# A deformable-attention block and three attention layers: a third folding step moved to DMA, and the MLP's first pixel block in seven products

## The chip, the cores and the metric

One core of one Trainium2 chip runs one program. The metric is device time in microseconds (us) of that core. A time is the median of several executions; a profile is one execution recorded by the hardware profiler. Engines: TensorE (PE, matmul), VectorE (DVE), ScalarE (ACT), GpSimd (POOL), SyncE (SP). Everything is float32.

## The reference, cut to what matters

The input is x, 2 x 512 x 32 x 32. Four layers follow one another: layer 0 is deformable attention and an MLP, layers 1 to 3 are attention layers on the same pixels. The change lies in layer 0 and in its MLP. There each of 8 groups of 64 channels has 64 sampled points (8 x 8) at learnt offsets, and the bias between each of 1024 pixels and each point comes from a small network:

```python
pos = grid_q[:, :, None, :] - grid_kv[:, None, :, :]          # 16 groups x 1024 pixels x 64 points x 2
bias = jnp.sign(pos) * jnp.log1p(jnp.abs(pos))
bias = jax.nn.relu(bias @ cpb_w1 + cpb_b1)                    # 2 -> 128
bias = jax.nn.relu(bias @ cpb_w2 + cpb_b2)                    # 128 -> 128
bias = (bias @ cpb_w3 + cpb_b3).reshape(b, GROUPS, H * W, Hd * Wd)
sim = jnp.einsum('bhid,bhjd->bhij', qh, kh) + bias
attn = jax.nn.softmax(sim, axis=-1)
...
x = x + out                                                   # attention, projected
xn2 = _bn(x, bn2_g, bn2_b)
h1 = gelu(einsum('bchw,oc->bohw', xn2, mlp_w1) + mlp_b1)      # 512 -> 2048
return x + einsum('bchw,oc->bohw', h1, mlp_w2) + mlp_b2       # 2048 -> 512
```

## The kernel before, in words

**Tiles and steps.** Layer 0 works on 8 tiles t (2 images x 4 pairs of groups). A tile has 128 points (two groups of 64) and 1024 pixels, and is done in 32 steps of four points, so the loop in `layer0` has 256 steps i. A step has four turns k = 0 to 3, each for one quarter (`part`) of the 128 hidden channels of the bias network, in the order 1, 0, 3, 2. Steps are numbered here within a tile too: "phase" is i modulo 32.

**What one turn issues.** `first` (L526, DVE) makes the first hidden layer of one point, 128 channels x 1024 pixels, from two tables; it works seven points ahead (`AHEAD`) in a ring of eleven buffers, eight of which are slices of the weight tile `wa`. `second` (L543, PE) multiplies the four points of the step by one quarter of `cpb_w2`, four points side by side in four groups of 32 columns, and ACT evicts with relu (L552). After the second and fourth turn, `joined` (L557, DVE) adds two quarters, so that after the next step's second turn a step has two arrays, and a DMA issued by POOL (L832) adds one to the other. A step is then one array of 128 partitions: 4 points x 32 sums of channels.

**Folding by DMA, two steps at a time.** At each even step a POOL DMA (L825) adds the odd partitions of an even step's array to its even ones, and at the odd step an SP copy (L827) and a POOL DMA (L829) put the odd step's two halves on top of each other in the freed odd partitions. Two steps are now one array of 8 points x 16 sums. `third` (L571, PE) sums those over the channels into `sim`, the scores of a tile: four such arrays per call, one in each group of 32 columns, for both halves of the pixels. A call covers 8 steps and comes 11 steps after the first of them: at phases 11, 19, 27 and, in the next tile, 3. The last of the four is followed by `scores` (L579) and by a new side queue.

**The side queue** `behind` holds what else a tile needs, as generators that are advanced by one `yield` at the second and fourth turn of each step: `finish(t)` (softmax of the scores, transposes `pt` L594 and `pa` L614), `offsets(t + 2)` (projection `pq` L328, 36 taps on ACT summed by six DVE reduces L353, then the tables), and `samples(t + 1)` (bilinear sampling `pk`, key and value products `pkv`, `pvo` L484, `pb` L488, `simbias` L490). The order of issue on each engine is the program's order (`in_order`). Matmul outputs outside of `sim` come from three PSUM buffers (`zt`), which `second` uses too.

**The end of layer 0 and the MLP.** `finish_last` does the softmax of the last tile in halves and the last projection of the image (`project_out` L629, `add_out` L639). `layers` begins with the MLP in 8 blocks of 256 pixels. Blocks 1 to 7 take seven products of half-size matrices for each eight (Strassen's scheme, Winograd's form: `lefts` and `rights` form the sums on DVE, `products` multiplies in PE with 128 columns, `combined` adds up). Block 0 is a plain product with 256 columns (`pmp`, L136), under which DVE forms the sums of w1 and w2 for the others.

Of the kernel before, what the change touches and what calls it, by code (L numbers as in the profile page):

```python
# [12 lines left out]
F32 = mybir.dt.float32  # L13
# [6 lines left out]
P = 128  # L20
# [12 lines left out]
RCH = 8  # L33
# [47 lines left out]
def kernel(ctx: ExitStack, tc: tile.TileContext, a: dict, out: bass.AP):  # L81
# [55 lines left out]

    def layer0(l0, fold_d, t2_b, o2_b):
# [5 lines left out]
        h2p = l0.enter_context(tc.tile_pool(name="att_h2", bufs=6))  # L144
        h2j = l0.enter_context(tc.tile_pool(name="att_h2j", bufs=3))
        h2b = l0.enter_context(tc.tile_pool(name="att_h2b", bufs=3))
        h2q = l0.enter_context(tc.tile_pool(name="att_h2q", bufs=3))
        dram = l0.enter_context(tc.tile_pool(name="l0dram", bufs=1, space=DRAM))
# [17 lines left out]
        qkw = h2j.tile([P, 2, NPAIR, P], F32, name="qkwbd", tag="h2")  # L166
# [58 lines left out]
        for w in (w3, w3_4):  # L225
            nc.gpsimd.memset(w, 0.0)
# [5 lines left out]
        def bias_weights():  # L232
# [3 lines left out]
            few = one.tile([P, 26], F32, name="few")  # L236
# [68 lines left out]
            nc.vector.tensor_scalar(w3[:, 24:32], w3[:, 24:32], w3sign[:, 1:2], None, ALU.mult)  # L305
            magnitude(b2h, w3_of)
# [14 lines left out]
        def offsets(t):  # L321
# [49 lines left out]
            if t:  # L371
                yield
            act = actbd[t % 2]
# [26 lines left out]
            yield  # L400
            sgn = two.tile([P, 2, 32], F32, name="sgn")
# [19 lines left out]
        def samples(t):  # L421
# [36 lines left out]
            yield  # L458

# [12 lines left out]
            yield  # L472
            pkv = zt([P, 2, P], "pkv")
# [9 lines left out]
            pvo = zt([P, C], "pvo")  # L483
            nc.tensor.matmul(pvo, values, ow, start=True, stop=True)  # L484
            vos[t] = vop.tile([P, C], F32, name="vo")
            nc.scalar.copy(vos[t], pvo)
            pb = zt([P, 1], "pb")
            nc.tensor.matmul(pb, kq, b1q[:, pr : pr + 1], start=True, stop=True)  # L488
# [4 lines left out]
        NCH = 2 * NR // RCH  # L493
        tabs_of = {}

        def load_tabs(c):
# [4 lines left out]
            for ax in range(2):  # L501
                src = slog_d[t, ax].rearrange("(q r) i -> q r i", q=4)
                tab = two.tile([P, 2, RCH, 32], F32, name=f"tab{ax}")
                q, r = rc % 2 * 2, rc // 2 * RCH
                nc.sync.dma_start(out=tab, in_=src[q : q + 2, r : r + RCH, :].partition_broadcast(P))
                tabs_of[c].append(tab)
# [8 lines left out]
        def first(p):  # L515

            chunk, quad = divmod(p, 2 * RCH)
            quad, point = divmod(quad, RCH)
            if quad == 0 and point == 0:
# [9 lines left out]
                in0=tx[:, quad, point, :].unsqueeze(1).to_broadcast([P, H, W]),  # L529
                in1=ty[:, quad, point, :].unsqueeze(2).to_broadcast([P, H, W]),  # L530
# [5 lines left out]
        def second(i, h1s, part):  # L536
# [13 lines left out]
            ring = h2q if part % 2 else h2b if part else h2j if i % 2 else h2p  # L550
            h2 = ring.tile([P, HW], F32, name="h2", tag="h2")
# [10 lines left out]
        def third(sim, r, h2s, fours=(), halves=range(2)):  # L562

            for half in halves:
                n = slice(half * HALF, (half + 1) * HALF)
                ways = [(quad, w3[:, 24 - r : 56 - r], h2) for quad, h2 in enumerate(h2s)]
# [16 lines left out]
        def finish(t, sim):  # L583
# [4 lines left out]
            simb = two.tile([P, HW], F32, name="simb", tag="simb")  # L588
# [10 lines left out]
            at = two.tile([P, 8, P], F32, name="at", tag="simb")  # L599
# [10 lines left out]
            nc.vector.tensor_tensor(atv, atv, sm.unsqueeze(2).to_broadcast([P, 16, NJ]), ALU.mult)  # L610
            yield
# [29 lines left out]
        def finish_last(sim, eights, fours):  # L641
# [3 lines left out]
            table(AF.Exp)  # L645
            pps = [zt([P, HW], "pp")]
            project_out(pps[0], b, 0, range(2))
            simb = two.tile([P, HW], F32, name="simb", tag="simb")
# [4 lines left out]
            pt = zt([P, 8, P], "pt")  # L653
            ptv = pt.rearrange("p i (g j) -> p (i g) j", j=NJ)
            mx = two.tile([P, 16], F32, name="mx")
            at = two.tile([P, 8, P], F32, name="at", tag="simb")
# [156 lines left out]
        for i in range(steps):  # L813
            for k, part in enumerate((1, 0, 3, 2)):
# [18 lines left out]
                if k % 2:  # L833
                    next(behind, None)
# [1391 lines left out]
```

## Time and profile before

| What | us |
|---|---|
| Median of three runs | 3383.11 (3380.47 to 3383.16) |
| The profiled execution, its own time | 3381.55 |
| Its span, first to last instruction | 3379.8 |
| PE busy, DVE busy, ACT busy, POOL busy | 3348.8, 2654.9, 1804.6, 464.7 |
| The loop of 256 steps | 57.7 to 2003.0 |
| One tile of the loop, from 501.68 to 742.01 | 240.33 |
| End of layer 0 (`finish_last`) | 2003.0 to 2042.1 |
| MLP block 0, then block 1 | 2043.39 to 2099.20, then to 2149.36 |

The granted clock of TensorE was 1.00 in every stretch that was looked at. A busy time is that in which an engine works on at least one instruction; waiting for a semaphore is idle time, and it is listed with the instruction that ended it. Instructions of PE overlap in the pipeline, so the time that one adds is read from the distance of starts, not from its own duration. A step of the loop that has nothing but its own `second` takes 6.87 us on PE (54.93 us for 512 instructions, 64 to a step: every float32 matmul is two instructions in the trace).

### The profile page before, as it was taken

Reading aid. Unit: us, or ns where it says so; the run is one execution under the profiler, and the core shown is the slowest. Engines: PE = TensorE matmul, PEld = TensorE weight load, DVE = VectorE, ACT = ScalarE, POOL = GpSimd, SP = SyncE. Lnnn points to the kernel's source line nnn. Section 1 sums busy time; section 2 is a strip of 40 time slices with the busy share of each in tenths; the row PEclk is TensorE's granted clock in tenths of the full one; section 3 lists DMA queues with packets and bytes.
Section 4 is the critical chain, followed back from the end, with each engine's and each line's share of the span. In section 5 each row is a group of like instructions: output and inputs, shape, how many; then the busy total and the mean of one; then the engine's idle time right before and its main releaser. Section 6 shows DMA issues by size and latency. Waiting matters only on the chain.

```text
span 3379.8 us, 61349 instructions
## 1 busy us (share of the span) xinstructions
PE 3348.8 (99%) x24861; PEld 1611.8 (48%) x24861; DVE 2654.9 (79%) x3458; ACT 1804.6 (53%) x2764; POOL 464.7 (14%) x563
## 2 busy tenths in 40 slices
PE   9999999999999999999999999999999999999999
PEld 4333333333333333333333337999953443687777
DVE  6999999999998899999999964464446566665656
ACT  4866867867866667867867651121226235122221
POOL 0222222222222122222222210000000000000000
PEclk9999999999999999999999999999999999999999
DMA  5676676676665476676676651000100000000111
GB/s 167 147 150 139 142 155 139 138 152 141 151 146 121 105 151 142 146 149 137 146 150 148 140 141 57 11 11 14 48 4 13 27 29 20 7 7 1 32 32 36
DMA packets 147284, 320.33 MB, mean 95 GB/s; under 512 B 31664, under 2 KB 77360, under 8 KB 146224
## 3 DMA queue, kind: packets, MB, share of 16 engines
q0 software_dynamic: 56880, 199.79, 31.1%
q1 hardware_dynamic: 88816, 111.81, 10.8%
q8 instruction: 198, 3.24, 0.4%
q10 hardware_dynamic: 1296, 4.72, 0.4%
q14 instruction: 94, 0.77, 0.1%
HBM read 71.46 MB, written 10.83 MB: 24 GB/s over the span
## 4 chain that ended last, share of the span: by engine, by line
PE 79%; DVE 15%; issue 4%; ACT 2%; DMA 0%; POOL 0%; DVEq 0%; SPq 0%; ACTq 0%; POOLq 0%
PE z L543 35%; DVE wa L526 6%; PE pw L1392 6%; PE pma L136 5%; PE pmb L136 4%; DVE h L557 4%; PE pmv L1392 4%; PE score L1571 3%; PE pv L1583 3%; PE pm L1392 3%; PE score L1392 3%; DVE h L526 2%; PE pmp L136 2%; PE pp L629 2%; PE pmt L1392 1%
## 5 line engine op out<-in xcount | busy, mean ns | idle before, releaser
L543 PE MATMUL z<-wa,cpb_w 128*32 128x512 f32 x11904 | 1779.1, 593 | 6.7 <-DVE simbias L490 3.4
L552 ACT ACTIVATE h<-z,b2h 128x1024 f32<-128x1024 f32 x1024 | 1134.9, 1114 | 529.1 <-PE z L543 505.7
L543 PE MATMUL z<-h,cpb_w 128*32 128x512 f32 x4480 | 986.3, 593 | 3.3 <-ACT h L552 2.2
L543 PEld LDWEIGHTS z<-wa,cpb_w 128*32 128x32 f32 x11904 | 493.0, 110 | 883.6 <-issue 804.2
L526 DVE CUSTOM_DVE_ANT_1 wa<-tab,tab 128x1024 f32<-128x1024 f32 x744 | 879.4, 1219 | 33.9 <-PE z L543 33.9
L557 DVE SCALAR_TENSOR_TENSOR h<-h,turn,h 128x1024 f32<-128x1024 f32 x512 | 654.7, 1279 | 8.8 <-ACT h L552 8.5
L543 PEld LDWEIGHTS z<-h,cpb_w 128*32 128x32 f32 x4480 | 256.3, 110 | 335.0 <-issue 292.0
L832 POOL DMA_DIRECT2D h<-h x255 | 227.2, 891 | 1062.4 <-DVE h L557 715.2
L526 DVE CUSTOM_DVE_ANT_1 h<-tab,tab 128x1024 f32<-128x1024 f32 x280 | 333.5, 1219 | 10.5 <-PE z L543 10.4
L1214 ACT COPY p<-pma 128x128 f32<-128x128 f32 x70 | 18.6, 266 | 305.5 <-PE pma L136 305.5
L1572 ACT ACTIVATE p<-score 128x512 f32<-128x512 f32 x256 | 130.0, 624 | 81.2 <-PE score L1571 80.4
L1206 DVE TENSOR_TENSOR upper<-pma,p 128x256 f32<-128x256 f32 x70 | 29.5, 422 | 163.4 <-ACT p L1214 163.3
L825 POOL DMA_DIRECT2D h<-h x126 | 109.6, 870 | 336.7 <-DMA h<-h 332.5
L829 POOL DMA_DIRECT2D h<-h x126 | 119.5, 948 | 133.0 <-DMA h<-h 126.7
L1604 DVE TENSOR_TENSOR acc<-acc,p 128x1024 f32<-128x1024 f32 x96 | 111.1, 1219 | 19.0 <-ACT p L1572 18.8
L1571 PE MATMUL score<-q,k 64*128 64x512 f32 x512 | 120.7, 604 | 1.1 <-DVE gm L1088 1.1
L1583 PE MATMUL pv<-p,vT 128*64 128x512 f32 x512 | 116.5, 598 | 0.0
L513 ACT ACTIVATE tab<-tab,pc 128x512 f32<-128x512 f32 x126 | 96.2, 763 | 0.0
L1392 PE MATMUL pmv<-wa,hc 128*128 128x256 f32 x384 | 89.7, 380 | 0.3 <-DVE u L1415 0.3
L347 ACT ACTIVATE products<-qpad,pc 128x64 f32<-128x64 f32 x252 | 85.5, 408 | 0.0
L1571 PEld LDWEIGHTS score<-q,k 64*128 64x128 f32 x512 | 47.3, 186 | 70.3 <-issue 54.9
L1392 PEld LDWEIGHTS pmv<-wa,hc 128*128 128x128 f32 x384 | 72.6, 190 | 14.2 <-issue 2.8
(451 smaller groups left out, 3708.5 us busy)
## 6 DMA issues: line engine op xcount, KB each, us to landing
h<-h POOLq DMA_DIRECT2D x255, 512.0 KB, 5.0
h<-h POOLq DMA_DIRECT2D x252, 256.0 KB, 4.8
tab<-slog_d SPq DMA_DIRECT2D x128, 256.0 KB, 4.5
h<-h SPq DMA_DIRECT2D x126, 256.0 KB, 2.3
r<-d SPq DMA_DIRECT2D x24, 256.0 KB, 3.5
xt<-in_xt SPq DMA_DIRECT2D x8, 512.0 KB, 7.8
wa<-in_mlp_w SPq DMA_DIRECT2D x4, 1024.0 KB, 7.8
wb<-in_mlp_w SPq DMA_DIRECT2D x16, 256.0 KB, 5.5
```

What stands on the lines that cost most here:

```text
L136: nc.tensor.matmul(pm, w, m, start=(k == 0), stop=(k == len(pairs) - 1))
L526: nc.vector._custom_dve(TENSOR_ADD_SAT, out=h1.rearrange("p (y x) -> p y x", x=W), in0=tx[:, quad, point, :].unsqueeze(1).to_broadcast([P, ...
L543: nc.tensor.matmul(z[point * 32 : point * 32 + 32, n], cpb_w2[:, lo : lo + 32], h1s[point][:, n], start=True, stop=True,)
L552: nc.scalar.activation(h2, z, AF.Relu, bias=b2h[:, part : part + 1])
L557: nc.vector.scalar_tensor_tensor(h2, h2, turn[:, part // 2 : part // 2 + 1], parts.pop(part + 1), ALU.mult, ALU.add)
L829: nc.gpsimd.dma_start(out=joins[i - 3][1:P:2], in_=joins.pop(i - 2)[1:P:2], accum_op=ALU.add)
L832: nc.gpsimd.dma_start(out=joins[i - 1], in_=other, accum_op=ALU.add)
L1392: nc.tensor.matmul(out, stationary(l, k), moving(r, k), start=start and k == 0, stop=k == nk - 1, skip_group_check=not start,)
L1571: nc.tensor.matmul(sc, ks[m][r, s * P : (s + 1) * P], qs[m][r, n], start=True, stop=True)
L1572: nc.scalar.activation(p[:, part], sc, AF.Exp, scale=64 ** -0.5)
L1583: nc.tensor.matmul(pv[half][part * 64 : part * 64 + 64], vt[s % 4][:, lo : lo + 64], lps[s, half][:, part, :], start=(s == 0), stop=(s == 7),)
L1604: nc.vector.tensor_add(acc[half], acc[half], ps[s, half])
```

## The change

Three things are changed together.

1. **A third fold.** Except for the last 16 steps of the last tile, four steps are put into one array of 16 points x 8 sums. Every step's array is folded once by POOL (256 KB); the first of four is folded again by POOL (128 KB), and each of the other three is brought in by an SP copy and a POOL DMA of 128 KB each. `third` is called once for 16 steps, with another weight tile (`w3_16`) but in the same eight matmuls, 20 steps after the first of them (phases 20 and, in the next tile, 4), ahead of the turn's `second`. The arrays that stay live (`h2p`, six) are slices of a new tile `bridge`, the passing ones (`h2j`) are four instead of three, two of them in `bridge`. A table load now brings 16 points of one quarter instead of 8 of two.
2. **The side queue's turns.** `finish`, `offsets` and `samples` have two more `yield`s each, `pb` moves into the PSUM buffer of `pvo` and ahead of it, and the queue starts half a step later.
3. **The MLP's block 0** goes the way of the others, in seven products. The sums of w1 are formed in `finish_last`, a column block after each of the eight `add_out`s, in slices 0 to 5 of `bridge`; the normalized pixels and their sums are made in slices 6 and 7, before the last exponentials. `finish_last` has two PSUM tiles for its transposes instead of one. The sums of w2 move into the second half of block 0; the loads and constants at the start of `layers` move behind its first lines.

```diff
+        h2p = cycle([bridge[:, k, :] for k in range(6)])
+        h2j = cycle([bridge[:, 6, :], bridge[:, 7, :], *(one.tile([P, HW], F32, name=f"h2j{k}") for k in range(2))])
...
+            quarter = few[:, 26:28]
+            for k in range(2):
+                nc.vector.tensor_reduce(quarter[:, k : k + 1], ident[:, 2 + k : P : 4], AX.X, ALU.add)
+                nc.vector.scalar_tensor_tensor(eighth, quarter[:, k : k + 1], 8.0, eighth, ALU.mult, ALU.add)
+            nc.vector.tensor_scalar(w3_16[:, 16:32], row[:, 0:16], eighth, 0.0, ALU.add, ALU.is_equal)
+            nc.vector.tensor_scalar(w3_16[:, 16:32], w3_16[:, 16:32], w3sign[:, 1:2], None, ALU.mult)
...
-            pvo = zt([P, C], "pvo")
-            nc.tensor.matmul(pvo, values, ow, start=True, stop=True)
+            pvo = zt([P, HW], "pvo")
+            pb = pvo[:, C : C + 1]
+            nc.tensor.matmul(pb, kq, b1q[:, pr : pr + 1], start=True, stop=True)
+            nc.tensor.matmul(pvo[:, :C], values, ow, start=True, stop=True)
...
-                if i < steps - 2:
-                    if i >= 2 and i % 2 == 0 and k == 0:
-                        nc.gpsimd.dma_start(out=joins[i - 2][0:P:2], in_=joins[i - 2][1:P:2], accum_op=ALU.add)
-                    if i >= 3 and i % 2 and k == 0:
-                        nc.sync.dma_start(out=joins[i - 3][1:P:2], in_=joins[i - 2][0:P:2])
-                    if i >= 3 and i % 2 and k == 3:
-                        nc.gpsimd.dma_start(out=joins[i - 3][1:P:2], in_=joins.pop(i - 2)[1:P:2], accum_op=ALU.add)
...
-                due = i - 11
-                if k == 1 and due >= 0 and due % 8 == 0:
+                due = i - 20
+                if k == 1 and 0 <= due < LAST and due % 16 == 0:
                     t, r = divmod(due, NR)
                     if r == 0:
                         sim = ps_s.tile([P, HW], F32, name="sim")
-                    third(sim, r, [joins.pop(due + j) for j in range(0, 8, 2)])
-                    if r == NR - 8:
+                    third(sim, r, [joins.pop(due + j) for j in range(0, 16, 4)], wide=True)
+                    if r:
...
+                if 0 <= i - 2 < LAST:
+                    j = (i - 2) % 4
+                    whole, own = joins[i - 2 - j], joins[i - 2]
+                    if k == 0:
+                        nc.gpsimd.dma_start(out=own[0:P:2], in_=own[1:P:2], accum_op=ALU.add)
+                    if k == 3 and j == 0:
+                        nc.gpsimd.dma_start(out=own[0:P:4], in_=own[2:P:4], accum_op=ALU.add)
+                    if k == 3 and j:
+                        nc.sync.dma_start(out=whole[j:P:4], in_=own[0:P:4])
+                if k == 1 and i - 1 in parts:
+                    other = joined(parts.pop(i - 1), 2)
+                    nc.gpsimd.dma_start(out=joins[i - 1], in_=other, accum_op=ALU.add)
+                j = (i - 3) % 4
+                if k == 1 and 0 <= i - 3 < LAST and j:
+                    nc.gpsimd.dma_start(
+                        out=joins[i - 3 - j][j:P:4], in_=joins.pop(i - 3)[2:P:4], accum_op=ALU.add
+                    )
...
+            pts = [zt([P, 4, P], "pt") for _ in range(2)]
             pps = [zt([P, HW], "pp")]
             project_out(pps[0], b, 0, range(2))
...
+            right_sums()
+            pps.append(ps_s.tile([P, HW], F32, name="pp", tag="sim"))
...
+            pps += [zt([P, HW], "pp") for _ in range(2)]
             for half, n in enumerate(halves):
-                for m in range(3):
-                    project_out(pps[m], b, m, range(NPAIR) if m == 2 else [pr], [half])
+                for m in range(CC):
+                    project_out(pps[m], b, m, range(NPAIR) if m >= 2 else [pr], [half])
                     add_out(b, m, n, pps[m])
+                    next(left_sums)
...
-            xn = normed(0)
-            hid = one.tile([P, HID // P, BLK], F32, name="hid")
-            for c in range(MC):
-                for m in (MC + c, c):
-                    pm = bank("pmp")[:, :BLK]
-                    accumulate(pm, [(w1[:, k, m * P : (m + 1) * P], xn[:, k, :]) for k in range(CC)])
-                    nc.scalar.activation(hid[:, m, :], pm, AF.Gelu, bias=col("mlp_b1", m))
-                form1(nc.vector, slice(c * P, (c + 1) * P))
...
-            for blk in range(1, NBLK):
+            nc.gpsimd.memset(ones, 1.0)
...
+            later = [form2(slice(c * P, (c + 1) * P)) for c in range(2)]
+            for blk in range(NBLK):
...
+                    if blk == 0 and c >= 4:
+                        advance(later[0])
...
+                if blk == 0:
+                    drain(chain(*later))
```

## The prediction, made before the changed kernel was run

> **What bounds the kernel now.** I read the page first (busy times, then the chain), then busy time by stretch, then the groups of one tile, then the two timelines side by side, and PE's waits last.
>
> ```profile
> PE 3348.8 (99%) x24861; PEld 1611.8 (48%) x24861; DVE 2654.9 (79%) x3458; ACT 1804.6 (53%) x2764; POOL 464.7 (14%) x563
> ...
> PE 79%; DVE 15%; issue 4%; ACT 2%; DMA 0%; POOL 0%; DVEq 0%; SPq 0%; ACTq 0%; POOLq 0%
> ```
>
> PE is the bound: every matmul removed should shorten the span. DVE's 15% of the chain is the warning: 79% is an average over two different stages. By stretch (span, then busy us of PE, PEld, DVE, ACT, POOL, clock, DMA share):
>
> ```profile
> 501.68:742.01 240.33, 239.07 (x2172) 74.52 (x2168) 232.99 (x213) 179.46 (x249) 56.01 (x66) 1.00 0.67 144
> 2000.00:2043.40 43.40, 39.08 (x141) 15.57 (x133) 12.97 (x17) 10.54 (x40) 0.94 (x4) 1.00 0.31 109
> 2043.39:2099.20 55.81, 55.81 (x258) 48.62 (x259) 24.68 (x48) 8.81 (x17) 4.01 (x7) 1.00 0.25 83
> 2099.20:2149.36 50.16, 50.16 (x451) 50.10 (x450) 23.26 (x75) 8.92 (x25) 2.31 (x4) 1.00 0.03 9
> ```
>
> In a tile of the loop DVE works 232.99 of 240.33 us, 6 us less than PE: a second bound close behind. The two MLP blocks differ by 5.65 us of pure PE. The end of layer 0 has 4.3 us of idle PE.
>
> ```profile
> L571 PE MATMUL sim<-h,w 128*32 128x512 f32 x64 | 7.6, 592 | 0.0
> ...
> 556.43 1.90 PE L571 MATMUL sim<-h,w 128*32 128x512 f32 x16
> ...
> 563.83 2.36 DVE L526 CUSTOM_DVE_ANT_1 wa<-tab,tab 128x1024 f32<-128x1024 f32 x2 [3.15 <-PE z L543]
> ...
> 668.18 2.36 DVE L526 CUSTOM_DVE_ANT_1 wa<-tab,tab 128x1024 f32<-128x1024 f32 x2
> 670.45 1.28 DVE L557 SCALAR_TENSOR_TENSOR h<-h,turn,h 128x1024 f32<-128x1024 f32 x1
> 671.64 2.36 DVE L526 CUSTOM_DVE_ANT_1 wa<-tab,tab 128x1024 f32<-128x1024 f32 x2
> ```
>
> The first line is the work to be halved. The DVE lines give its pace: 2.27 us from start to start for two `first`, 1.19 for a `joined`, so 2 x 2.27 + 2 x 1.19 = 6.92 us a step against PE's 6.87. Where PE inserts something, DVE waits for a free buffer (3.15).
>
> ```profile
> PE z L543 <- ACT h L552: 5.4, 11, 0.7
> PE z L543 <- DVE simbias L490: 4.5, 8, 0.6
> ...
> PE pmp L136 <- POOL xn L1224: 1.3, 1, 1.3
> ...
> PE pt L662 <- DVE mx L663: 0.9, 1, 0.9
> PE pp L629 <- DVE x L639: 0.8, 1, 0.8
> PE sim L571 <- ACT simb L652: 0.8, 1, 0.8
> ...
> PE pt L679 <- ACT at L669: 0.5, 1, 0.5
> ```
>
> **The thirds: what goes.** 31 calls in the loop become 16, each still eight matmuls (16 records). PE's step starts give the price: a step with a `third` and nothing else takes 8.58 us, a plain one 6.87, so 1.71 (the group's 1.90 overlaps its neighbours). 15 x 1.71 = **-25.7 us**, about 3.4 a tile.
>
> **Does DVE allow it?** I take as lead the start of PE's first `second` of a step less the end of the DVE instruction that made its fourth point. It is capped at 5.45 plus what PE inserts in the step before, by the ring of eleven; a plain step costs it 0.06, each of the six reduces 0.95, and what PE inserts adds to it. In the tile at 501 it reads 6.3 at phase 12, then 5.35, 4.4, 3.45, 2.5, 2.0, 1.9, 1.8 at phase 19, where a `third` lifts it: PE never caught up. With the new phases the balance is: 5.0 at phase 4; `third`, `scores` and `pt` there (3.76 + 1.16) lift it, the cap cuts it back to 5.4; `pa` and `pq` (1.1, 2.0) at 9 and 10 make good the softmax's 1.5 on DVE; 5.4 at phase 13. The reduces fall at 12 to 17, so 4.4, 3.5, 2.5, 1.6, 0.6, and 0.1 at 19 (`po` adds 0.42); no `third` at 11 helps any more, the next is at 20, and then it is 1.6. So PE catches up for about a step: 0.3 us each in six tiles, and 0.5 in the first, where the lead is 0.7 to 1.1 already at steps 8 to 11. **+2.3 us** (0 to 12, if it starts 1.5 lower). A tile then asks 236 us of PE, still over DVE's 233.
>
> **The third fold: what it adds.** For four steps: before 4 DMAs of 512 KB, 4 of 256 by POOL, 2 of 256 by SP; after 4 of 512, 4 of 256 and 4 of 128 by POOL, 3 of 128 by SP. So 12 POOL issues for 8, 3968 KB for 3584, and a DMA share near 0.75 for 0.67. POOL's row:
>
> ```profile
> L832 POOL DMA_DIRECT2D h<-h x33 | 29.4, 892 | 131.8 <-DVE h L557 78.1 <-DMA h<-h 26.0 <-DVE simbias L490 7.8
> ...
> h<-h POOLq DMA_DIRECT2D x255, 512.0 KB, 5.0
> h<-h POOLq DMA_DIRECT2D x252, 256.0 KB, 4.8
> ```
>
> At 0.9 us an issue POOL needs 2.7 of 7.4 us a step. The page SBUF — State Buffer of the Trainium skill (section "SBUF: two separate sides") speaks against more of this: POOL writes the descriptors of its DMAs through ports that a DVE operation in a two-port mode locks, and the page tells of 620 ns becoming 3100. Three issues of 3.1 would be 9.3 us a step: some 240 x 1.7 = +410 us. The row has a mean of 0.89 with DVE busy 97%, so I count 0.9. What counts more is POOL's order. At turn 0 it waits for the last step's 512 KB to land, to fold it; the next 512 KB addition, the 128 KB addition and (one step in four) the second fold are queued behind. The cycle is an issue of 0.87 plus a landing of 5.0, 5.9 us, under PE's shortest step of 6.87. The last 128 KB lands some 4.5 steps after its step began, against 5.25 for the `third` that needs it: 5 us to spare, 2 where DVE is late. The buffers of `h2j` come back after five steps, with about as much. A 128 KB addition isn't in the trace: between the SP copy's 2.3 and the 4.8 of 256 KB; I take 4, the nearer row's kind. SP's copies wait for a fold with the tables' loads queued behind, and these have four steps' time. **+1 us** (0 to 15, one a `third`).
>
> **The side queue.** `pb` no longer holds a PSUM buffer alone until DVE reaches `simbias`: -4 of the 4.5 us of that wait. The 5.4 us for ACT sit mostly at phase 5 (two waits of 0.4 and 0.5), where table load, tables and exponentials meet; the extra turns thin them out, but the table load comes nearer to the tables' scaling. I count 0 (-5 to +3). **-4 us.** The six small DVE operations for `w3_16`, 0.2 each by the small rows, lie in the start under PE's folding of weights: **+0.5** (0 to 1.2, uncovered).
>
> **The end of layer 0.** Separate transposes' tiles remove half of the 0.9 and the 0.5; `pp` waits no more for `add_out` (0.8); xn is ready in time (1.3): its POOL work (2.2) starts when the second half of `third` has read the slice, and DVE's 1.7 of sums follow before the first reciprocal. Against this, the first projection gets the third PSUM buffer, which ACT frees at 2004.3 where PE stood ready at 2003.0: +1.4. The w1 sums, 1.5 us behind each `add_out` of 0.8 on DVE, take 8 x 2.3 = 18.4 us against PE's 17.8 of projection; w1 landed at 2015, ten us before. DVE ends 2 us after PE, and block 0 first asks DVE after 3 us of products. Without the slack it would be these 2. **-1.7 us** (-3.1 to +1).
>
> **Block 0.** The page TensorE: Matmul & The Clock Gate of the skill (section "Back-to-back issue gap") speaks against halves of 128 columns: it gives some 81 ns a matmul at 128 columns and 131 at 512, about 98 at 256 by a line between (my estimate), so 448 x 81/98 against 256: 45% more, +25 us. The rows say 50.16 / 448 = 112 ns against 55.81 / 256 = 218, near half: block 1 is the same work, and I take it. The sums of w2 (8 operations of some 1.2 us on DVE) fit in 25 us of idle DVE; w2 landed 15 us after its issue, and in the new order its last chunk comes when the fifth column block is done, without PE waiting. **-5.65 us** (-5.7 to -3).
>
> **Sum.** -25.7 + 2.3 + 1 - 4 + 0.5 - 1.7 - 5.65 = -33.2 from the profiled execution's 3381.55 (span 3379.8 and 1.75 around it) is 3348.3; that execution is 1.6 below the median, so 3350.
>
> **The rivals.**
> - *Half of the loop's gain comes back as waits.* For it: the lead at 0.1, and DVE, POOL and DMA all fuller. Against it: PE asks 3 us a tile more than DVE. Six tiles at 1.7 more and fifteen `third`s at 0.4: +16, **3366**.
> - *All idle PE in the loop goes.* A tile has 1.26 of it, 9.5 in all instead of 4; no wait at the first projection, no lost lead: -9, **3341**.
> - *Slower: POOL's cycle becomes the bound.* Fold, addition and landing are one chain, and each step now has it. A tenth of the 512 KB additions land after more than 6.7 us, those beside a fold or a table load; 128 KB more in flight, at the 0.8 between 512 and 256 KB by rows, is 0.4: 7.1, a cycle of 8.0 against 7.6 for a mean step (1945 us / 256). 240 x 0.4 - 7 = +89, **3470**. It decides from a mean landing of 6.8 us; the median of 5.0 is against it.
> - *The fold isn't fewer matmuls*: 240 records stay. The code's calls say otherwise; **3376**.
>
> **Chances.** The forecast 0.62 (3343 to 3357), the waits 0.24, no idle 0.08, POOL 0.04, no fewer matmuls 0.02. A change under 0.2% (6.8 us) can't be told from none. Faster 0.94, same 0.03 (the last and a mild POOL case), slower 0.03. The range runs from 3338 to 3367, with both neighbours in.
>
> **What would show it.** L571 in the loop with 256 records for 496 (and 24 in `finish_last`); a plain tile of 236 to 237 us, DVE over 98% busy in it; PE waits for DVE only at phases 18 to 20; `simbias` gone from PE's waits; L832's landing under 6 us; block 0 at 50.2 us, starting within 2 us after the last projection. Wrong, if PE waits for DMA at `third`, or if a tile stays over 239.

## The result, and the profile after

The changed kernel takes **3350.03 us** (median of 6; 3348.83 to 3353.46) against 3381.39 (6; 3380.3 to 3383.16) of the kernel before, run beside it: a ratio of 0.9909, 95% interval 0.9896 to 0.9922. On another chip it took 3350.88 (4; 3349.33 to 3352.67) beside 3381.73.

The profiled execution, 3353.46 with a span of 3351.7, is the slowest of its six. The differences below are between the profiled spans, 3379.8 and 3351.7: -28.1. The medians differ by 31.4.

The page after, busy times and then the chain that ended last:

```profile
PE 3323.8 (99%) x24813; PEld 1611.7 (48%) x24813; DVE 2673.0 (80%) x3540; ACT 1805.5 (54%) x2774; POOL 676.7 (20%) x804
...
PE 82%; DVE 9%; issue 5%; DMA 2%; ACT 1%; POOL 1%; DVEq 0%; SPq 0%; POOLq 0%; ACTq 0%
```

PE lost 25.0 us of busy time. DMA, at 0% of the chain before, now has 2%; DVE has 9%, where it had 15%.

By stretch (span, then busy us of PE, PEld, DVE, ACT, POOL, clock, DMA share): a tile of the loop, the end of layer 0 after its last `second`, block 0, block 1.

```profile
555.48:793.67 238.19, 237.11 (x2141) 74.46 (x2137) 232.47 (x213) 179.41 (x249) 83.14 (x97) 1.00 0.79 158
1982.15:2019.76 37.61, 35.60 (x113) 15.07 (x109) 22.80 (x49) 8.60 (x38) 2.39 (x5) 1.00 0.29 113
2019.76:2071.17 51.41, 50.51 (x449) 50.25 (x450) 33.27 (x87) 10.31 (x26) 3.52 (x4) 1.00 0.27 88
2071.17:2121.30 50.13, 50.13 (x450) 50.07 (x449) 24.94 (x80) 9.19 (x26) 2.55 (x4) 1.00 0.04 12
```

The tile took 238.19 us, not 236 to 237, with DVE busy for 97.6% of it, not over 98: both engines had idle time. The five plain tiles took 236.88 to 239.20 us. Block 0 is 1.3 us longer than block 1, the same products.

The thirds' matmuls (`third` is L645 now; records, then ns of one):

```profile
L645 PE MATMUL sim<-bridge,w x276: 592/592/617, 208.7 to 1990.9; 128*32 128x512 f32 x138
...
L645 PE MATMUL sim<-h2j,w x4: 592/592/593, 1986.7 to 1990.9; 128*32 128x512 f32 x4
```

276 + 4 are the 256 + 24 that were to be there, so the fold is fewer matmuls. PE's waits:

```profile
PE z L616 <- ACT h L625: 5.3, 10, 0.6
PE pqb L261 <- DMA cpb_w<-in_cpb_w: 3.3, 1, 3.3
...
PE sim L645 <- DMA bridge<-bridge: 1.5, 2, 1.3
...
PE pma L1338 <- ACT hid L1303: 0.9, 1, 0.9
PE pma L135 <- POOL ones L1292: 0.9, 1, 0.9
PE sim L645 <- ACT simb L729: 0.8, 1, 0.8
```

`simbias` is gone from the list, as is `add_out`. The first line looks as before (5.4 us in 11 waits), but these are other waits. Before, most sat at phase 5, one in each tile. Now they come twice in each of five tiles, at the ends of phases 18 and 21, with two causes. The chain, pieces in order of time (start, us, what):

```profile
661.37 1.27 DVE h L630
...
663.46 2.34 DVE wa L599 x2
665.80 1.21 DVE bridge L630
...
667.09 1.12 ACT h L625
...
668.26 8.79 PE z L616 x80
...
690.74 0.22 ACT near L505
...
691.31 0.07 ACT tab L587
...
691.83 1.10 ACT h L625
...
692.97 7.05 PE z L616 x61
```

Up to 668.26, the end of phase 18, `first` (L599) and `joined` (L630) on DVE set the pace, and PE follows through ACT's eviction: DVE's lead has run out, a step before the `third` at phase 20 that would lift it. At 692.97, the end of phase 21, it is ACT itself: the sampling's weights (`near`, L505) and the scaling of a table (L587) stand ahead of the eviction.

And `third` itself can be late, here in the next tile, where its first six records had run and the other ten waited:

```profile
797.71 1.90 PE L645 MATMUL sim<-bridge,w 128*32 128x512 f32 x10 [1.29 <-DMA bridge<-bridge]
```

Where the 28.1 us went. Within the loop a stall is what a step of PE takes over the shortest step with the same matmuls in it, in any of the kernels run here; a step with `third` and `gpb`, for one, is 9.34 at its shortest. This takes in waits in the middle of a call, of which the list of waits shows a part only (1.5 us for DMA at the thirds; by steps it is 6.7). So measured, the loop of the kernel before has 11.7 us of stalls, the changed kernel's 18.9. Block 0 runs from its first product to the first of block 1, which in the kernel before starts at 2099.08, not 2099.20.

| Part (profiled spans) | Predicted | Measured |
|---|---|---|
| 15 thirds less, 1.71 each | -25.7 | -25.7 |
| DVE's lead runs out: phase 18, 0.7 in each of five tiles | +2.3 | +3.4 |
| PE waits for DMA at a third: 4.1 at phase 4, 2.6 at phase 20 | +1 | +6.7 |
| `pb` within `pvo`, 0.49 a tile | -4 | -3.9 |
| Old waits gone: phase 5 (5.1 to 0.7), phases 9, 21 and 23 (4.2) | 0 | -8.7 |
| New waits: ACT at phase 21 (3.8), phase 27 (0.8), first tile (1.1) | 0 | +5.7 |
| Loop, not placed | 0 | -0.3 |
| Loop in all (first `second` to first `pp` of `finish_last`: 1945.35 to 1922.58) | -26.4 | -22.8 |
| Start | +0.5 | +1.9 |
| End of layer 0 (40.38 to 37.61) | -1.7 | -2.8 |
| Block 0 (55.69 to 51.41) | -5.65 | -4.3 |
| What follows | 0 | -0.2 |
| Sum | -33.2 | -28.1 |

In the profiled execution on the other chip (span 3348.4) the waits of the loop came again, with 3.4 us for the lead, 5.2 for DMA and 3.8 for ACT at phase 21. The start is another matter: in the profiles of the thirteen runs that have the changed start (the changed kernel twice, and its edits) it took 56.6 to 59.7 us, 58.4 in the mean, against 57.7 in the one profile of the kernel before. So most of the +1.9 is scatter, and what the six small operations cost isn't shown.

### The profile page after: what moved, and what is told of

The parts are those of the page before. It is cut to its first block, busy times and chain, and to the rows that moved or that the text cites. A ratio compares the mean times of both kernels' runs of the same rounds, so it can differ in the third digit from the quotient of the medians.

```text
span 3351.7 us, 61808 instructions
## 1 busy us (share of the span) xinstructions
PE 3323.8 (99%) x24813; PEld 1611.7 (48%) x24813; DVE 2673.0 (80%) x3540; ACT 1805.5 (54%) x2774; POOL 676.7 (20%) x804
## 4 chain that ended last, share of the span: by engine, by line
PE 82%; DVE 9%; issue 5%; DMA 2%; ACT 1%; POOL 1%; DVEq 0%; SPq 0%; POOLq 0%; ACTq 0%
PE z L616 38%; PE pma L135 6%; PE pw L1435 6%; PE pmb L135 5%; PE pmv L1435 4%; PE score L1614 3%; PE pv L1626 3%; DVE wa L599 3%; PE pm L1435 3%; PE score L1435 3%; PE pmt L1435 1%; PE ppr L1435 1%; DVE h L599 1%; DMA bridge<-h 1%; DVE bridge L630 1%
## 5 line engine op out<-in xcount | busy, mean ns | idle before, releaser
L625 ACT ACTIVATE h<-z,b2h 128x1024 f32<-128x1024 f32 x768 | 851.3, 1114 | 347.9 <-PE z L616 310.6
L599 DVE CUSTOM_DVE_ANT_1 wa<-tab,tab 128x1024 f32<-128x1024 f32 x744 | 878.1, 1216 | 1.3 <-PE z L616 1.1
L599 DVE CUSTOM_DVE_ANT_1 h<-tab,tab 128x1024 f32<-128x1024 f32 x280 | 332.9, 1216 | 2.3 <-PE z L616 2.2
L630 DVE SCALAR_TENSOR_TENSOR h<-h,turn,h 128x1024 f32<-128x1024 f32 x256 | 326.8, 1276 | 4.3 <-ACT h L625 4.3
L625 ACT ACTIVATE bridge<-z,b2h 128x1024 f32<-128x1024 f32 x162 | 180.8, 1116 | 121.4 <-PE z L616 119.0
L927 POOL DMA_DIRECT2D bridge<-bridge x150 | 127.6, 850 | 547.2 <-DMA bridge<-h 510.5
L630 DVE SCALAR_TENSOR_TENSOR bridge<-bridge,turn,h 128x1024 f32<-128x1024 f32 x162 | 206.8, 1277 | 4.2 <-ACT bridge L625 4.2
L934 POOL DMA_DIRECT2D bridge<-h x161 | 163.4, 1015 | 213.2 <-DVE h L630 123.6
L927 POOL DMA_DIRECT2D h2j<-h2j x90 | 76.2, 847 | 323.0 <-DMA h2j<-h 293.6
L625 ACT ACTIVATE h2j<-z,b2h 128x1024 f32<-128x1024 f32 x94 | 105.0, 1117 | 37.9 <-PE z L616 37.3
L630 DVE SCALAR_TENSOR_TENSOR h2j<-h2j,turn,h 128x1024 f32<-128x1024 f32 x94 | 120.0, 1276 | 0.0
L937 POOL DMA_DIRECT2D bridge<-h2j x90 | 111.9, 1244 | 2.6 <-issue 1.8
```

The costliest lines, as they stand in the source:

```text
L599: nc.vector._custom_dve(TENSOR_ADD_SAT, out=h1.rearrange("p (y x) -> p y x", x=W), in0=tx[:, point, :].unsqueeze(1).to_broadcast([P, H, W] ...
L625: nc.scalar.activation(h2, z, AF.Relu, bias=b2h[:, part : part + 1])
L630: nc.vector.scalar_tensor_tensor(h2, h2, turn[:, part // 2 : part // 2 + 1], parts.pop(part + 1), ALU.mult, ALU.add)
L927: nc.gpsimd.dma_start(out=own[0:P:2], in_=own[1:P:2], accum_op=ALU.add)
L934: nc.gpsimd.dma_start(out=joins[i - 1], in_=other, accum_op=ALU.add)
L937: nc.gpsimd.dma_start(out=joins[i - 3 - j][j:P:4], in_=joins.pop(i - 3)[2:P:4], accum_op=ALU.add)
```

## The experiments

Each is an edit of the changed kernel, timed beside the kernel before, whose medians in these comparisons are 3380.45 to 3381.93; so the medians of the edits are set beside the changed kernel's 3350.03. The intervals of the ratios of `queue_later`, `third_later` and `later_both` overlap with the changed kernel's; their slowest times are 1.4 us or more under its fastest, and the rest is read from the stalls in the traces.

**One part each**

`mlp_only`: part 3 alone. The loop's folds, its `third`s at phases 11, 19, 27 and 3, the turns and `pb` are as before.

```diff
-        LAST = NT * NR - 16
+        LAST = 0
...
-                due = i - 20
...
+                if k == 1 and due >= 0 and due % 8 == 0:
...
-            pvo = zt([P, HW], "pvo")
-            pb = pvo[:, C : C + 1]
...
-                yield
```

> The changed kernel with part 3 alone (block 0 in seven products, the new end of layer 0); the loop is as before: two steps to an array, a third every 8 steps, the side queue's turns and pb as before. Theory, from the two profiles: the end of layer 0 gives 2.8 us and block 0 gives 4.3, and the two parts add up: 7 us faster than before, a ratio of 0.998. Rival: part of what the profiles show there is the loop's tail (the last DMA landings are earlier in the changed kernel), and alone the part gives 4 us or less.

3374.21 us (3373.26 to 3376.36) against 3381.18; ratio 0.9981, 0.9973 to 0.9988. -7.0 for block 0 and the end of layer 0, as the two lines of the table have it (-7.1).

`no_third_fold`: parts 2 and 3. The loop folds and sums as before.

```diff
-        LAST = NT * NR - 16
+        LAST = 0
...
-                due = i - 20
-                if k == 1 and 0 <= due < LAST and due % 16 == 0:
...
+                if k == 1 and due >= 0 and due % 8 == 0:
...
+                    third(sim, r, [joins.pop(due + j) for j in range(0, 8, 2)])
```

> Parts 2 and 3 without part 1: the loop folds two steps to an array as before, third every 8 steps at the old phases, but the side queue has its added turns and pb its new place. Theory: the turns take PE's waits for ACT and simbias away whether or not the third fold is there (0.5 + 0.64 + 0.3 us in seven tiles), and DVE's lead doesn't run out because there is a third at phase 11: 8 to 10 us faster than part 3 alone, 3364 to 3367, 0.9955 to 0.996; the third fold on top of it is then worth 15 us, not 26. Rival: the turns only pay with the third fold, which crowds the queue: 3372 to 3375, 0.998.

3369.85 us (3369.3 to 3372.15) against 3380.45; 0.9971, 0.9959 to 0.9982. That is -10.6, so the turns and `pb` bring 3.6 us over `mlp_only`: the prediction's -4, and about all of it `pb`'s. PE waits as much for ACT as before:

```profile
PE z L616 <- ACT h L625: 5.7, 12, 0.7
```

By phases, stalls of 1.8 us go at phase 5 and 3.5 come at phase 21; in all they are 11.7, as in `mlp_only`. On top of parts 2 and 3 the third fold brings 31.4 - 10.6 = 20.8 us, of a price of 25.7.

`no_turns`: parts 1 and 3. The six added `yield`s go, and `pb` has its own buffer again.

```diff
-            pvo = zt([P, HW], "pvo")
-            pb = pvo[:, C : C + 1]
-            nc.tensor.matmul(pb, kq, b1q[:, pr : pr + 1], start=True, stop=True)
-            nc.tensor.matmul(pvo[:, :C], values, ow, start=True, stop=True)
+            pvo = zt([P, C], "pvo")
+            nc.tensor.matmul(pvo, values, ow, start=True, stop=True)
...
+            pb = zt([P, 1], "pb")
+            nc.tensor.matmul(pb, kq, b1q[:, pr : pr + 1], start=True, stop=True)
```

> The changed kernel without part 2's yields and with pb in a PSUM buffer of its own again; third fold and block 0 stay. Theory: PE's waits that part 2 took away come back in each of seven tiles (0.5 at pb, 0.64 for ACT behind pt, 0.3 at pk), 10 us slower than the changed kernel, a ratio to before of 0.994. Rival 1: only pb counts, as the prediction had it, 4 us, 0.992. Rival 2: the DMA chain sets the pace of the loop anyway and hides these waits: 0.991.

3357.61 us (3356.67 to 3359.28) against 3381.18; 0.9931, 0.9917 to 0.9944: 7.6 slower than the changed kernel. Its PE waits show what comes back:

```profile
PE z L611 <- ACT h L620: 9.8, 16, 1.2
PE z L611 <- DVE simbias L551: 4.8, 8, 0.6
...
PE pk L135 <- ACT h L620: 1.6, 1, 1.6
```

By phases the stalls are 6.5 us at phase 17 (`actbd`, a table and `th` stand on ACT ahead of an eviction there), 3.6 at 5 and 1.5 to 2.1 each at 8, 12 and 19. Next to none is left at the thirds (0.2 us at one of them), and none for the lead at phase 18. So the changed kernel's turns do two things: they thin out the places where the side queue's work stands on ACT ahead of an eviction, and they bring in the waits for the lead and at the thirds. The new waits cost nearly what the old ones did: in all, this loop has 19.6 us of stalls, against 18.9 with the turns (17.4 in the profile on the other chip). Of the 7.6 us, 3.9 are `pb`'s, as in the table; the added `yield`s account for 0.7 to 2.2, and the rest isn't placed.

**The price of a third**

`third_twice`: the eight matmuls of each wide `third` are issued once more, with a weight tile of zeros.

```diff
+        w3_no = one.tile([P, 32], F32, name="w3_no")
...
+                if wide:
+                    ways += [(quad, w3_no, h2) for quad, h2 in enumerate(h2s)]
```

> The changed kernel with every wide third's eight matmuls issued a second time with weights of zero: PE has all the work back that the third fold takes from it, and the DMAs stay. Theory: PE is the bound and a call costs 1.71 us: 15 of them are 25.7, less what they save of PE's waits after phase 20 (some 5): 20 to 26 us slower than the changed kernel, a ratio to before of 0.997 to 0.9985. Rival: the DMA chain is the bound in the loop, PE has slack there, and the matmuls cost under 8 us: below 0.993.

3375.61 us (3373.87 to 3379.47) against 3381.18; 0.9985, 0.9978 to 0.9992: +25.6 for 15 times 16 records more.

```profile
L648 PE MATMUL sim<-bridge,w_no x240: 592/592/617, 208.5 to 1919.4; 128*32 128x512 f32 x120
```

1.71 us a call holds: the shortest step with a doubled `third` takes 10.30 us, for 8.58. What the whole kernel pays is less certain. Between the two profiled executions the loop grew by 21.4 us only, as its stalls fell from 18.9 to 14.5: those at phase 4 are gone, so there the added matmuls seem to have filled time in which PE was idle. The medians, 25.6 apart, don't show this, but the runs of this kernel scatter over 5.6 us.

**DVE's lead**

`queue_later`: the side queue starts one turn of the queue (half a step) later.

```diff
                         behind = chain(
+                            iter([None]),
                             finish(t, sim),
```

> The changed kernel with the side queue started one turn pair (half a step) later, so that each of its pieces moves from the fourth to the second turn of a step or the other way. Theory: DVE's lead is cut to 3.3 us at phases 6 and 28 because mx and simbias, which wait for PE's fourth turn, stand just ahead of the next first; moved to the second turn they leave the lead at 5.4, DVE doesn't run out in the six reduces, and PE's waits at phases 18 and 20 (0.7 and 0.76 a tile) go: 7 to 9 us faster than the changed kernel, a ratio to before of 0.988 to 0.989. Rival: POOL's chain of fold, addition and landing is the floor by now, what PE doesn't wait for DVE it waits for DMA at third: 0.991, with PE's waits for bridge doubled.

3343.99 us (3341.97 to 3344.92) against 3381.18; 0.9888, 0.9873 to 0.9903: 6.0 faster than the changed kernel. Its lead is 4.5 to 4.7 us at phases 7 to 10 (the changed kernel: 2.7 to 3.2), 5.4 at 13 (4.6) and 0.8 at 18 (0.0); it still runs out, a step later, at 19. Its stalls are 13.1 us for 18.9: the lead costs 1.2 for 3.4, ACT at phases 21 and 22 2.5 for 3.8, and DMA 3.2 for 6.7, as none is left at phase 20, probably because where DVE is earlier, so are the DMAs behind it. Phase 5 costs 1.4 more. The trace shows in DVE's order why the lead is lower without it. In the changed kernel, DVE around phases 4 and 5 (start, us, instruction, and in brackets the idle time before it), then the end of PE's step at phase 4:

```profile
561.56 2.35 DVE L599 CUSTOM_DVE_ANT_1 wa<-tab,tab 128x1024 f32<-128x1024 f32 x2
567.83 1.23 DVE L671 TENSOR_REDUCE mx<-pt 128x16 f32<-128x1024 f32 x1 [3.92 <-PE pt L668]
568.97 1.28 DVE L630 SCALAR_TENSOR_TENSOR bridge<-bridge,turn,h 128x1024 f32<-128x1024 f32 x1
570.16 2.35 DVE L599 CUSTOM_DVE_ANT_1 wa<-tab,tab 128x1024 f32<-128x1024 f32 x2
```

```profile
566.17 0.59 PE L616 MATMUL z<-h,cpb_w 128*32 128x512 f32 x1
566.70 1.09 PE L668 MATMUL pt<-cst,simb 128*128 128x128 f32 x8
```

`mx`, the maximum of the softmax, needs PE's transposes and stands right ahead of `joined` and the next `first`. DVE waits 3.92 us for it. In the first 2.85 of these the ring is full in any case: the next `first` needs a buffer that PE reads until 566.76, the end of this step. But the `joined` behind `mx` would have fitted into that wait, and from 566.76 on the ring is free while DVE still stands at `mx`, then does `mx` and `joined`: the next `first` starts at 570.16, 3.4 us after its buffer was free.

**The DMA at the third**

`third_later`: `third`, `scores` and the queue come a whole step later (phases 21 and 5), except near the end.

```diff
-                due = i - 20
+                due = i - (20 if i >= 244 else 21)
```

> The changed kernel with the wide third (and with it scores and the side queue) 21 instead of 20 steps after its first step; only the last one stays at 20. Theory: in the changed kernel's profile PE waited up to 2.3 us for the last 128 KB addition at some of the thirds, 6 us in all; one step more is enough for it to land, and the time falls by 3 to 6 us against the changed kernel: 3344 to 3347, 0.989 to 0.990. Rival: the DMA chain sets the pace, and the wait only moves to the next buffer: 3349 to 3351, 0.991.

3347.15 us (3345.39 to 3347.41) against 3381.93; 0.9895, 0.988 to 0.991: 2.9 faster; its loop is 5.7 us shorter in the profiled execution. No wait of PE for `bridge` is left at any third, nor one for the lead at phases 18 to 20. But 4.8 us of new stalls stand at phase 9, where ACT's exponentials now meet its scaling of the tables, 0.7 a tile.

`later_both`: this and `queue_later` together.

> The third at 21 steps and the side queue half a step later, both. Theory: the two waits of PE (for DVE after the six reduces, for DMA at third) have separate causes, and the gains add up: 6 us of the queue and 3 to 5 us of the third, 3339 to 3341, a ratio to before of 0.988. Rival: one bound, the DMA chain, stands behind both: not better than the queue alone, 3343 to 3344, 0.9888.

3345.57 us (3345.31 to 3345.67); 0.9892, 0.9877 to 0.9907: not better than `queue_later` alone. The waits at the thirds are gone, but phase 9 has 5.1 us, and the stalls are 13.3 in all, as in either kernel alone:

```profile
PE z L616 <- ACT h L625: 4.6, 9, 0.7
```

`small_first`: POOL issues the 128 KB addition ahead of the 512 KB one of the same turn.

```diff
-                if k == 1 and i - 1 in parts:
-                    other = joined(parts.pop(i - 1), 2)
-                    nc.gpsimd.dma_start(out=joins[i - 1], in_=other, accum_op=ALU.add)
...
+                if k == 1 and i - 1 in parts:
+                    other = joined(parts.pop(i - 1), 2)
+                    nc.gpsimd.dma_start(out=joins[i - 1], in_=other, accum_op=ALU.add)
```

> The changed kernel with the 128 KB addition ahead of the 512 KB addition of the same turn in POOL's order. Theory: POOL's chain (fold, 512 KB addition, its landing) is within half a microsecond of a step's time; an issue of 0.9 us ahead of the 512 KB addition lengthens every step's chain to 7.4 us or more, against 7.3 for a step, and what the earlier landing of the 128 KB saves at third is lost: 0 to 10 us slower than the changed kernel. Rival: the chain has slack, and the 128 KB piece, no longer queued behind 512 KB, lands 3 us earlier: PE's waits for it vanish, 3 to 5 us faster.

3351.07 us (3346.4 to 3355.03); 0.9904, 0.9889 to 0.9919: no difference. The landing did what was meant. First the changed kernel, then this one (median us from issue to landing; the line holds the second folds too), and this one's wait:

```profile
bridge<-bridge POOLq DMA_DIRECT2D x150, 128.0 KB, 5.4
```

```profile
bridge<-bridge POOLq DMA_DIRECT2D x150, 128.0 KB, 3.6
```

```profile
PE sim L645 <- DMA bridge<-bridge: 3.7, 2, 3.1
```

For the 128 KB additions alone, it is 5.9 and 3.8. In this profiled execution (the slowest of four) the stalls at phase 20 are gone, but those at phase 4 are 8.1 us for 4.1, and new ones at phase 11 come to 4.9:

```profile
PE z L616 <- ACT qpad L391: 3.8, 4, 1.5
```

So the place in the queue sets the landing, but other waits took over, and what makes phase 4 late here stays open. The trace of the changed kernel has a hint: ahead of each of its six late thirds SP had issued a table load (256 KB) 8.3 to 9.0 us before, and the last additions were issued while it was under way; of the nine that were on time, two had one as near. No run moves the table load alone, so this is a coincidence in time, not a cause shown.

**Is POOL's chain near its bound?**

`one_more`: in three of four steps POOL issues one more DMA of 128 KB, behind the fold and on partitions that nobody reads any more.

```diff
+                    if k == 3 and j:
+                        nc.gpsimd.dma_start(out=own[1:P:4], in_=own[3:P:4], accum_op=ALU.add)
```

> The changed kernel with one more POOL DMA of 128 KB in three of four steps, which adds dead partitions of the same array to each other (no result depends on it) and waits for the step's fold as the second fold does. This is a price for what the third fold added to POOL and the DMAs. Theory: the chain is close to its bound, 0.9 us of issue and 128 KB more bring it to 7.5 us or over, and thirds wait: 10 to 40 us slower than the changed kernel, 3360 to 3390. Rival: POOL and the DMAs have slack to spare (20% and some 75% busy), under 3 us.

3352.83 us (3351.7 to 3354.11); 0.9913, 0.9899 to 0.9926: +2.8, not clear of no difference. The stalls at phases 4 and 20 are 9.7 us for 6.7, so the 180 more issues and landings make the thirds 0.2 us later each, and nothing else:

```profile
PE sim L645 <- DMA bridge<-h: 2.6, 2, 1.6
```

The idea that the chain fold, addition, landing is close to the step's length fell.

**Both mended**

`half_step`: `third`, `scores` and the queue start in the fourth turn of the same step, two turns later, instead of the second.

```diff
-                if k == 1 and 0 <= due < LAST and due % 16 == 0:
+                if k == (1 if i >= 244 else 3) and 0 <= due < LAST and due % 16 == 0:
```

> The changed kernel with the wide third, scores and the start of the side queue in the fourth turn of the same step instead of the second (the last one stays): the queue's pieces are then where queue_later has them, and the DMAs have half a step (3.4 us) more, without moving the exponentials onto the steps in which ACT scales the tables, which cost later_both 0.7 us a tile at phase 9. Theory: the gain of queue_later (6 us) and what is left of PE's waits for DMA there (3 to 6 us): 3338 to 3342, a ratio to before of 0.987 to 0.988. Rival: the two gains don't add up for a reason that isn't this one: 3344 to 3346, 0.989.

3341.72 us (3340.58 to 3343.64) against 3380.45; 0.9884, 0.9869 to 0.9899: 8.3 faster than the changed kernel. A tile of the loop, and DVE around its phases 4 and 5:

```profile
554.76:790.86 236.10, 235.99 (x2141) 73.97 (x2136) 232.74 (x213) 179.28 (x249) 83.42 (x97) 1.00 0.79 158
```

```profile
565.60 2.36 DVE L599 CUSTOM_DVE_ANT_1 wa<-tab,tab 128x1024 f32<-128x1024 f32 x2 [1.61 <-PE z L616]
567.88 1.27 DVE L630 SCALAR_TENSOR_TENSOR h<-h,turn,h 128x1024 f32<-128x1024 f32 x1
570.08 1.23 DVE L671 TENSOR_REDUCE mx<-pt 128x16 f32<-128x1024 f32 x1 [0.92 <-PE pt L668]
```

PE has 0.1 us of idle time in the tile, and 236.10 is inside the prediction's 236 to 237. DVE stands still for 1.61 + 0.92 us, not 3.92: it does the `joined` ahead of the wait, goes on with `first` as soon as a buffer is free, and comes to `mx` later. The steps at phase 4 take 10.63 in every tile and those at phase 20 take 8.58, so no `third` waits for a DMA. The stalls of the loop are 8.8 us, fewer than before the change. The page's chain says the same:

```profile
PE 91%; DVE 3%; issue 2%; ACT 2%; DMA 1%; POOL 0%; SPq 0%; DVEq 0%; ACTq 0%; POOLq 0%
```

The times of `half_step` and `queue_later` do not tell the two apart. The trace does: `queue_later` has 3.2 us of waits for DMA at phase 4.

**Block 0, and the two kernels side by side**

`changed_again` is the changed kernel as it is; `half_step_w2` is `half_step` with all eight sums of w2 behind the column blocks of block 0.

```diff
-                    if blk == 0 and c >= 4:
-                        advance(later[0])
```

> The changed kernel as it is, on the chip of the next kernel, so that the two can be set side by side. Expected 3350 us (3347 to 3353).

> The third, the scores and the queue start in the step's fourth turn, and none of the eight sums of w2 stands between block 0's column blocks: all eight follow the last of them. Theory: the sums between the column blocks (1.22 to 1.42 us each on DVE) hold back the last Gelu, and PE waits 0.9 us for it; behind the last block the sums of the first four take 4.9 us, and the first product that needs one of them comes after three others of about 1.8 us each, so PE does not wait: block 0 takes 50.5 instead of 51.4, the wait for ACT hid goes, and the time is 3340.8. Rival: the wait is the end of the chain product, addition, Gelu, which is there without the sums too: block 0 stays at 51.4 and the time at 3341.7. Third: the sums now come too late for the product that needs them, and PE waits for DVE instead: 52 to 54 and 3342 to 3344. Against the changed kernel on the same chip I expect 8 to 10 us less, with intervals apart.

On one chip, the changed kernel took 3350.88 us (3349.33 to 3352.67; 0.9911, 0.9894 to 0.9927) and the other 3341.91 (3340.86 to 3343.11; 0.9884, 0.9868 to 0.9901): 9.0 faster. The two intervals overlap by a hair, as each carries the scatter of the runs of before; of the times themselves, the slowest of the one is 6 us under the fastest of the other.

But block 0 took 51.34 us, no less than 51.41. The changed kernel first (all engines, around the last column block), then this one:

```profile
2045.52 1.42 DVE L161 TENSOR_TENSOR wb<-wb 128x1024 f32<-128x1024 f32 x1
...
2048.22 0.51 ACT L1302 ACTIVATE hid<-hid,pc 128x256 f32<-128x256 f32 x1 [2.05 <-DVE hid L1272]
2048.63 0.49 ACT L1303 ACTIVATE hid<-upper,pc 128x256 f32<-128x256 f32 x1
...
2049.18 0.71 PE L1338 MATMUL pma<-hid,wb 128*128 128x128 f32 x4 [0.90 <-ACT hid L1303]
```

```profile
2032.99 3.88 PE L1336 MATMUL pma<-hid,wb 128*128 128x128 f32 x32
...
2036.70 1.95 PE L135 MATMUL pma<-hid,wb 128*128 128x128 f32 x16
...
2036.94 1.23 DVE L161 TENSOR_TENSOR w2s<-wb 128x1024 f32<-128x1024 f32 x1
2038.20 1.23 DVE L161 TENSOR_TENSOR w2s<-w2s,wb 128x1024 f32<-128x1024 f32 x1
...
2039.48 2.05 PE L135 MATMUL pma<-hidt,w2s 128*128 128x128 f32 x16 [0.83 <-DVE w2s L161]
```

The theory was half right: without the sums the last Gelu is in time and that wait is gone, so they do hold it back. But I had taken three products as cover for the sums. Three do lie ahead of the one that needs the second sum (32 + 16 records), but two of them are done at 2036.87, before DVE has finished the last column block and starts on the sums at 2036.94. So one product covers two sums, and PE waits 0.83 us for DVE instead. Two sums between earlier column blocks and the rest behind might avoid both; this wasn't tried.

## Why the prediction was right, and where its steps were not

The time came out as predicted, 3350. DMA was off by +5.7, block 0 and the start together by +2.7, the lead by +1.1; the side queue's waits for ACT, put at nothing, gave -3.0 back, and the end of layer 0 -1.1. In the profiled spans the sum was 5 us short; that execution lies 3.4 above its median. That 3350 was met to a tenth is luck, then: errors of both signs cancel in part, and the forecast was reckoned from a median of 3383.11, while the kernel before took 3381.39 in this comparison. The gain by medians was 31.4 us, not 33.1.

- **The thirds, -25.7: right.** The count is exact, and doubling them cost 25.6 by medians (21.4 in the loop of the profiles, where stalls fell).
- **The lead, +2.3: about right, by a lower lead.** 3.4 us, in five tiles instead of seven, and within the phases 18 to 20 that were named ("PE catches up for about a step"). But the lead was 3.1 at phase 4 in most tiles, not 5.0, and 3.3 at phase 6 and 4.6 at 13, not 5.4: "the cap cuts it back to 5.4" failed. It looked at how many buffers DVE may fill, not at what DVE's own order lets it do: `mx` stands there with its wait. So it reached 0 a step earlier and cost 0.7 a tile, not 0.3; that the sum is near is in part luck.
- **The DMA at the third, +1: too low, within its bound.** The 4 us for the 128 KB addition failed. It took the size as what matters, between SP's copy and POOL's 256 KB. The addition stands directly behind one of 512 KB and lands just after it, a median of 5.9 us from its issue, and six of fifteen thirds waited, up to 2.3 us. "2 where DVE is late" fits the three at phase 20, where DVE had 0.1 us of lead left (0.8 to 0.9 us of wait each); the three at phase 4 had a lead of 3.1 or more, and their cause stays open. The row of the 512 KB additions (5.0) was the nearer one. `one_more` made this wait longer and `half_step` took it away. It was one of the two signs named for a wrong prediction; of the five plain tiles one was over 239 (239.2), the other sign. Both meant a few us here, not the forecast.
- **The side queue, -4: right for `pb`** (-3.9; parts 2 over part 3 brought 3.6). For ACT I counted 0, with -5 to +3; old waits of 8.7 us went and new ones of 5.7 came, -3.0. The turns did thin out the waits at phase 5, and the tables' scaling did come into the way, at phase 21, as said; the same shift is seen again at phase 9 of `third_later`.
- **The end of layer 0, -1.7: -2.8.** The +1.4 for the first projection's PSUM buffer did not occur; `pp` starts right behind the last `second`. The w1 sums stayed hidden. Block 0 began 0.89 us after PE was ready. The profile puts this wait down to POOL's memset of `ones`, but that had ended 0.49 us before PE started; the last `add_out` on DVE ended only 0.10 us before, at 2019.66, and is the likelier one.
- **Block 0, -5.65: -4.3.** That the sums of w2 "fit in 25 us of idle DVE" failed. The idle time is there, but between the column blocks it lies ahead of a Gelu that PE needs, and behind them, in `half_step_w2`, one product is less cover than two sums need. Block 1 at 50.13 us, and PE's 50.51 in block 0, bear out the rows, and not the estimate of +25 us that the prediction made from the page's sustained figures (the Trainium skill, TensorE: Matmul & The Clock Gate, "Back-to-back issue gap"): here 448 records of 128 columns took 50.13 us, against 55.69 for 256 of 256 columns.
- **POOL's cycle, the slower rival: refuted.** The 512 KB additions land after a mean of 5.80 us, against the 6.8 from which it decides, and `one_more` added to the chain for +2.8. The share of the DMA engines in a tile rose to 0.79, not 0.75. Nor did POOL's issues become 3 us with DVE 97.6% busy. The 3100 ns for 620 of the Trainium skill (SBUF — State Buffer, "SBUF: two separate sides") are for a DMA beside DVE operations in a two-port mode, and no run here shows whether those of this loop use one. Of the rows of POOL's DMA issues (busy us and mean ns, then idle before) the highest mean is

```profile
L937 POOL DMA_DIRECT2D bridge<-h2j x90 | 111.9, 1244 | 2.6 <-issue 1.8
```

- **"Half of the loop's gain comes back as waits", 3366:** in part. Its 0.4 a third came (6.7 / 15 = 0.45), its 1.7 more a tile for the lead did not (0.7 in all). "All idle PE in the loop goes", 3341, is the time that `half_step` reached, with 0.1 us of idle PE in a tile.

## What to carry to other kernels

How far an engine can run ahead is not set by its free buffers alone: an instruction that waits for another engine, in the same in-order queue, stops everything behind it (here `mx`, for 3.92 us). Look where such an instruction stands when the engine it waits for is busiest; moving it by half a step, and the deadline of the DMAs with it, was worth 8 us here. And before a deadline is set by a transfer's landing, look at what is ahead of it in its queue, and not at its size alone: the same 128 KB took 5.9 us or 3.8.

## What the runs showed of the hardware that was not expected

A 128 KB addition by DMA, issued by POOL right behind one of 512 KB, landed after a median of 5.9 us (from the start of its issue), longer than the first fold of 256 KB that goes alone (3.3); ahead of the 512 KB it took 3.8, and those hardly changed (5.5 and 5.7). Whichever of the two was issued second also took longer to issue: the 128 KB one 1.24 us second and 1.07 first, the 512 KB one 1.03 first and 1.27 second. SP's copy of 128 KB landed after 3.7 us, where the 256 KB copy of the kernel before took 2.3.
